# A new order for the first five units, and sums and a norm that leave GpSimd

## The chip, the cores and the metric

The kernel runs on one core of a Trainium2 chip. The metric is the device time of one execution in microseconds (us). Engines are called by their names in the profile: PE (TensorE matmul), PEld (its weight loads), DVE (VectorE), ACT (ScalarE), POOL (GpSimd) and SP (the queue that issues all DMAs of this kernel).

## The reference, cut to what matters

A transformer block on 16 sequences of 256 tokens with 256 features: an attention with 16 heads of 128, and a gated feed-forward layer of width 2048 whose weights come as packed 4-bit codes with scales. Each half is normalised at both ends.

```python
def _layernorm(x):                       # eps 1e-5
    return (x - mean(x)) / sqrt(var(x) + eps)

def attn(x):                             # x: 16 x 256 x 256
    q, k, v = (einsum('bpd,hde->bphe', x, W) + b for W, b in ...)
    s = einsum('bqhe,bkhe->bhqk', q, k) / sqrt(128)
    a = softmax(where(causal, s, -1e5))
    z = einsum('bkhe,bhqk->bqhe', v, a)
    return einsum('bqhe,hed->bqd', z, W_O) + b_O

def ffn(x):                              # Wg, Wu, Wd: 4-bit codes times scales
    gate, up = x @ Wg.T, x @ Wu.T
    return (gelu_tanh(gate) * up) @ Wd.T

x = x + _layernorm(attn(_layernorm(x)))
x = x + _layernorm(ffn(_layernorm(x)))
```

## The kernel before, in words

**Precision.** TensorE multiplies in fp32r. To keep fp32 accuracy, operands are split into a high part (a copy to fp32r) and a low part (value minus high part). A product takes three matmuls (`mm3`): high by high, low by high and high by low. So nearly every operand costs a copy on ScalarE (the high part) and a subtraction on VectorE or GpSimd (the low part): `kh`/`kl`, `qh`/`ql`, `vh`/`vl`, `ph`/`pl`, `zh`/`zl`, `inter`, and the weights.

**Attention.** The 4096 tokens are cut into `NBLK` = 8 blocks of 512 (two sequences). For each block there are 8 pairs of heads, and a *unit* is one head of one block: 128 units. The loop `for i in range(-5, N + 2)` is a software pipeline over units; step `i` runs, in this order, stages of different units:

- `st_s(i+4)`: scores of both sequences into the two `sc` banks; four masked minima on VectorE in place; the waiting `vl` (kept in the list `after`); four exponentials on ScalarE, which read the `sc` banks; reciprocals `rc`; four scalings `pr` on GpSimd.
- `st_qk(i+5)`: the products `pk` and `pq` (six matmuls each, one PSUM bank each), then `kh`, `kr`, `qh`, `qr` on ScalarE and `kl`, `ql` on VectorE.
- `st_t(i+4)`: the block transpose `tr` of `pr` on VectorE.
- `st_o`, `st_z(i)`, `st_p(i+1)`: the output product `po`, the product `pz` with the values, and the split of the transposed probabilities `ph`, `pl`.
- `st_v(i+4)`: the value product `pv` of four heads for one quarter of the tokens. There is one `pv` bank; ScalarE copies it to `vh` (or `vr`), and for the first two of four quarters VectorE forms `vl`, which is put on the list `after` and issued by the next `st_s`, behind its masks.
- `st_b`, `st_w`: the DMA hop through HBM that completes the transpose (`hop`, `pt`).

In the first five steps (`i` = -5 to -1) there is no `pz` and no `po`, so TensorE has only `sc`, `pk`, `pq` and `pv`.

**Order on each engine.** The helper `run` (line 99) records each instruction behind the last one of every engine, so on each engine the program's order is the order in which it runs; all instructions have line 99 in the profile, and groups are told apart by tile names. The DMAs are recorded in order as well (line 91).

**Side work.** Jobs that are not part of the pipeline (weight splits, norms, weight decoding, operand sums) are generators in lanes: `splits`, `urgent`, `behind`, `made`, `spare`, `idle`. A job says with `yield V_`, `A_`, `G_` or `N_` on which engine its next piece runs. A `slot(kinds)` takes one piece of the first lane whose next piece is of that kind and due. `add` puts a job into a lane, `await_` and `finish` drain one.

- `mid(b, oT)`: the end of attention for a block. It turns the output, loads it (`o`), measures it (`ln_stats`: VectorE, with one power on GpSimd), normalises it (`att`, four pieces), adds the input (`xs`, two sums), stores it to `x1d`, measures again, normalises again (`xn`, four pieces) and hands the turned tokens on for the feed-forward stage.
- `x_ops(sb)`: for each pair of blocks (`NSB` = 4 pairs), the operands of the feed-forward products. The stage uses Winograd's form of Strassen's method: seven block products (`m1` to `m7`) instead of eight, with sums of the four input blocks. `less` makes a sum, `put` splits one (a copy on ScalarE and a subtraction).
- `end(b, tr)`: the end of the feed-forward half for a block: norm on ScalarE in place in `o`, and the residual sum into `X1`, four sums of 256 columns.

**Feed-forward stage.** From about 1035 us on a loop runs over 32 groups `k` (4 pairs of blocks by 8 slices of the width). A group takes 15 us, with the products `pa`, `pf`, `pd`, `pe` for gate and up (`g`, `u`), the sums and the gelu that turn them into `inter`, and four down products `st_d` of the group before. It has five places with `slot(V_)` followed by `slot(A_ + G_)`.

At the start 30 transposes (`keep_warm(30)`) into a scratch bank keep TensorE busy before the first tokens have come, with 3 and 6 more among the first real ones.

Of the kernel before, what the change touches and what calls it, by code (L numbers as in the profile page):

```python
# [28 lines left out]
def kernel(  # L29
# [30 lines left out]
    def f(ap):  # L60
        return ap.bitcast(F32)
# [24 lines left out]
    def dma(dst, src):  # L86
        if queue[0] is None:
            queue[0] = nc.sync.dma_start(dst, src).ins
            return
        with tc.issue_after(queue[0]):  # L90
            queue[0] = nc.sync.dma_start(dst, src).ins
# [3 lines left out]
    def run(op, dst, *args, **kw):  # L95
        with ExitStack() as behind:
            for m in last.values():
                behind.enter_context(tc.issue_after(m))
            ins = op(dst, *args, **kw)  # L99
        last[ins.ins.engine] = ins.ins  # L100
        return ins
# [49 lines left out]
    def half(t, b, hf):  # L151
        r = b * TB + hf * S
        return t[r : r + S, :].rearrange("(t p) d -> p t d", p=P)
# [18 lines left out]
    def pairs_of_h(ap, out):  # L172
        return ap.rearrange("p (two h) -> p two h" if out else "p (h two) -> p two h", two=2)

    def ln_apply(dst, src, mv, rs, t):
        run(nc.gpsimd.tensor_scalar, dst, src, mv[:, t, 0:1], rs[:, t : t + 1], ALU.subtract, ALU.mult)
# [17 lines left out]
    def wide(name):  # L194
        return work.tile([P, 4, D], F32, tag="wide", name=name, bufs=4)
# [135 lines left out]
    def w_get(p, n):  # L331

        if p < NG:
            add(splits, split(p, n), A_ if n in "vo" else V_)
        elif p < len(pairs):
            overdue(now[0] + 4)
            if n == "v":
                key, part = p // 2, p % 2
                w = HALF.pop(key) if part else w_tile(n)
                HALF[key] = w  # L340
                dma(f(w[:, part]), WD[key % (NG // 2), n][:, part])
                if part:
                    W[key, n] = w_view(HALF.pop(key))
            else:
                w = w_tile(n)
                dma(f(w), WD[p % NG, n])
                W[p, n] = w_view(w)
# [200 lines left out]
    def cols4(ap):  # L548
        return ap.rearrange("p (h k j) -> p h k j", h=2, k=4)
# [3 lines left out]
    def mid(b, oT):  # L553

        tr = back_tile()
        back(tr, 0, oT[:, 0])
        yield V_
        back(tr, 1, oT[:, 1])
        yield N_, 2
        o = yield from back_load(tr)  # L560
        xs = [x_load(x, b, hf) for hf in range(2)]
        yield V_, 8
        xt = [xs[t // 2][:, t % 2, :] for t in range(4)]
        mv, rs = yield from ln_stats(o)
        att = wide("att")
        for t in range(4):
            yield G_
            ln_apply(cols4(att[:, t, :]), o[t], mv, rs, t)
        for hf in range(2):
            yield G_  # L570
            run(nc.gpsimd.tensor_tensor, xs[hf], xs[hf], att[:, 2 * hf : 2 * hf + 2, :], ALU.add)
        yield V_
        mv, rs = yield from ln_stats(xt)
        for hf in range(2):
            dma(half(x1d, b, hf), xs[hf])
        xn = wide("xn")
        for t in range(4):
            yield G_
            ln_apply(pairs_of_h(xn[:, t, :], True), pairs_of_h(xt[t], False), mv, rs, t)
        yield V_  # L580
        HOP2[b] = dram.tile([P, 4, 2 * P], F32, name=f"xhop{b}")
        yield from turn_tokens(HOP2[b], xn)
        ready.add((0, b))
# [108 lines left out]
    def x_ops(sb):  # L692

        xr = []
        for b in (2 * sb, 2 * sb + 1):
            xr.append(wide("xr"))
            dma(xr[-1], HOP2[b])
        yield A_, 8

        def block(kt, bb):  # L700
            return xr[bb].rearrange("p a (m i) -> p m a i", m=8)[:, 4 * kt : 4 * kt + 4]

        def four(ap):
            return ap.rearrange("p (t a i) -> p t a i", t=4, a=4)

        ops = X[sb] = {}

        def put(name, hi, lo, src):
            run(nc.scalar.copy, four(hi), src)
            run(nc.gpsimd.tensor_tensor, four(lo), src, f(four(hi)), ALU.subtract)  # L710
            ops[name] = hi, lo

        def pair():
            t = work.tile([P, 2, 2, TB], F32R, tag="xT", name="xT", bufs=4)
            return [(t[:, 0, k], t[:, 1, k]) for k in range(2)]

        def less(o, a, b):
            run(nc.gpsimd.tensor_tensor, o, a, b, ALU.subtract)

        x11, x12, x21, x22 = block(0, 0), block(0, 1), block(1, 0), block(1, 1)  # L720
        p1, p2 = pair()
        put("11", *p1, x11)
        yield A_
        put("21", *p2, x21)
        yield G_
        t1, t3, t4 = x11, x12, x21
        less(t1, x12, x11)
        yield G_
        less(t3, x22, x12)
        yield G_  # L730
        t2 = four(sb_tile("raw", "xsum", 6))
        less(t2, x22, t1)
        yield A_
        p1, p2 = pair()
        put("t2", *p1, t2)
        yield G_
        less(t4, t2, x21)
        yield A_
        put("t1", *p2, t1)
        yield A_  # L740
        w = w_tile("k")
        put("t3", w[:, 0], w[:, 1], t3)
        yield A_
        w = w_tile("q")
        put("22", w[:, 0], w[:, 1], x22)

        def last_one():
            hi = work.tile([P, TB], F32R, tag="ph", name="xh")
            lo = work.tile([P, TB], F32R, tag="pl", name="xl")
            put("t4", hi, lo, t4)  # L750

        if sb == 0:

            ops["last"] = last_one
        else:
            yield A_
            last_one()

    def sb_tile(tag, name, bufs):
        return work.tile([P, TB], F32, tag=tag, name=name, bufs=bufs)  # L760
# [127 lines left out]
    def end(b, tr):  # L888
        o = yield from back_load(tr)
        yield V_, 8  # L890
        mv, rs = yield from ln_stats(o)
        yield V_
        nb = ln_shift(mv, rs, 4)
        for t in range(4):
            yield A_
            run(nc.scalar.activation, o[t], o[t], AF.Identity, bias=nb[:, t : t + 1], scale=rs[:, t : t + 1])
            to = cols4(X1[b][t // 2][:, t % 2, :])
            run(nc.gpsimd.tensor_tensor, to, to, o[t], ALU.add)
        yield N_, 2
        for hf in range(2):  # L900
            dma(half(out, b, hf), X1[b][hf])
# [86 lines left out]
    def keep_warm(count):  # L988
        for n in range(count):
            run(nc.tensor.transpose, warm[:, n % 4, :], ident, ident)  # L990

    keep_warm(30)
    add(urgent, first, V_)
    finish(urgent)
    run(nc.gpsimd.tensor_scalar, bqs, bqk[:, 0, :], qscale, 1.0, ALU.mult, ALU.mult)
    for p in range(2):
        w_split(p, "v")
    for p, n in (2, "v"), (1, "k"), (1, "q"):
        w_get(p, n)

    def weights(*of):
        for pn, n in of:
# [3 lines left out]
    for i in range(-5, N + 2):  # L1006
        p = i // 2
        odd = i % 2 == 1
        if p >= 0 and not odd and p < len(pairs):
            b, g = pairs[p]  # L1010
            if g == 0 and b + 1 < NBLK:
                add(urgent, ln1(b + 1), N_)
            if b == 0 and g == 6:
                pieces = [(fg, n) for fg in range(NG) for n in "gud"]
                f_load(*pieces[0])
            if b == 0 and g == 7:
                for m, piece in enumerate(pieces):
                    add(idle, f_make(*piece, pieces[m + 1] if m + 1 < len(pieces) else None), V_)
            if b == NBLK - 1 and g == 0:
                add(spare, x_ops(0), N_)  # L1020
        if 0 <= i + 4 < N:
            st_s(i + 4)
        slot(V_)
        if i + 5 < N:
            st_qk(i + 5)
        slot(V_, urgent, behind)
        slot(G_)
        slot(G_)
        if 0 <= i + 4 < N:
            st_t(i + 4)  # L1030
        if i == N:
            X[0].pop("last")()
        if i >= N - 4:
            part(0, ("m1", "m2", "m6", "m5", "m7", "m3")[i - (N - 4)])
        if 0 <= p - 1 < len(pairs):
            st_o(p - 1, i % 2)
        if 0 <= i < N:
            st_z(i)
        if 0 <= i + 1 < N:
            st_p(i + 1)  # L1040
        if 0 <= i + 4 < N:
            st_v(i + 4)
        elif after:
            run(*after.popleft())
        if 0 <= i + 3 < N:
            st_b(i + 3)
        if 0 <= i + 4 < N:
            st_w(i + 4)
        if odd:
            weights((p + 1, "o"), (p + 5, "v"))  # L1050
        else:
            weights((p + 4, "k"), (p + 4, "q"))
        slot(A_ + G_)
        if N - 9 <= i < N - 7:
            f_get(0, "ug"[i - (N - 9)])
# [97 lines left out]
```

## Time and profile before

| | before |
|---|---|
| time, median of 3 runs | 1522.82 us (1521.78 to 1523.2) |
| profiled execution | 1522.04 us |
| its span in the profile | 1520.3 us |
| PE busy | 1501.7 us (99%) |
| PEld / DVE / ACT / POOL busy | 1278.5 / 1175.9 / 1033.9 / 810.3 us |
| DMA | 407.55 MB, mean 268 GB/s |
| granted PE clock, mean | 0.999 |

The profile shows one execution. Times in it are counted from the start of the span. "Idle before" is the idle time of an engine just before an instruction, with the instruction that ended it behind an arrow. A row of the timeline gives start, duration, engine, line, operation, output and inputs, shapes and count; rows of a group by shape give count, busy time, mean of one in ns, and idle time before. A table by stretch gives each engine's busy time in it with the number of instructions, then the granted clock of TensorE, the share of DMA time and the GB/s.

### The profile page before, as it was taken

The numbers are of one execution on the slowest core, as the hardware profiler recorded it, in microseconds if no ns is written. First come the engines' busy times: TensorE is split into PE (matmuls) and PEld (weight loads), VectorE is DVE, ScalarE is ACT, GpSimd is POOL, SyncE is SP. The second block draws the span as 40 slices with busy tenths as digits, with TensorE's granted clock in tenths as the row PEclk, the third lists the DMA queues.
The fourth block names the chain that finished last, engine by engine and source line by source line (L and its number), as shares of the span: only waits on it lengthen the run. The fifth ranks groups of instructions, "written<-read, shape, count | busy, mean of one in ns | idle before, by whom it ended". The sixth has DMA issues, their size and how long they took to land.

```text
span 1520.3 us, 25782 instructions
## 1 busy us (share of the span) xinstructions
PE 1501.7 (99%) x7831; PEld 1278.5 (84%) x7831; DVE 1175.9 (77%) x2950; ACT 1033.9 (68%) x2606; POOL 810.3 (53%) x1018
## 2 busy tenths in 40 slices
PE   8999999999999999999999999999999999999997
PEld 7888888888888888888888888887788878878886
DVE  6876787787787888788778777777877777787766
ACT  6886776777676677676776767675666665666565
POOL 3754578677667776866876876882320230140100
PEclk9999999999999999999999999999999999999999
DMA  8998899999889899899899999976547465645551
GB/s 287 336 317 266 263 310 298 294 299 317 281 291 329 280 322 311 265 322 299 280 287 304 312 304 316 310 247 254 219 180 276 185 232 195 254 174 201 216 232 57
DMA packets 200427, 407.55 MB, mean 268 GB/s; under 512 B 21472, under 2 KB 128480, under 8 KB 189536
## 3 DMA queue, kind: packets, MB, share of 16 engines
q1 hardware_dynamic: 200288, 405.91, 79.6%
q8 instruction: 62, 1.02, 0.3%
q14 instruction: 77, 0.63, 0.1%
HBM read 294.15 MB, written 111.67 MB: 267 GB/s over the span
## 4 chain that ended last, share of the span: by engine, by line
PE 89%; DVE 5%; ACT 4%; DMA 1%; issue 1%; POOL 1%; POOLq 0%; ACTq 0%; SPq 0%; DVEq 0%
PE pd L99 11%; PE pk L99 11%; PE po L99 11%; PE pv L99 11%; PE pq L99 11%; PE pz L99 10%; PE sc L99 9%; PE pa L99 7%; PE pf L99 5%; DVE sum L99 3%; PE pe L99 2%; DVE inter L99 1%; ACT inter L99 1%; ACT part L99 1%; ACT o L99 1%
## 5 line engine op out<-in xcount | busy, mean ns | idle before, releaser
L99 POOL TENSOR_SCALAR pr<-pr,rc 128x128 f32<-128x128 f32 (+1 forms) x512 | 250.2, 504 | 89.9 <-DVE rc L99 89.9
L99 ACT ACTIVATE pr<-sc,mn 128x128 f32<-128x128 f32 (+1 forms) x512 | 208.2, 419 | 87.2 <-DVE mn L99 87.0
L99 POOL TENSOR_TENSOR pl<-pt,ph 128x512 fp32r<-128x512 f32 x128 | 165.0, 1289 | 190.1 <-ACT ph L99 181.8
L99 DVE CUSTOM_DVE_ANT_0 sc<-sc,mask 128x128 f32<-128x128 f32 (+1 forms) x512 | 180.6, 373 | 67.8 <-PE sc L99 59.1
L99 PE MATMUL pv<-wv,xT 128*128 128x512 f32 x768 | 208.9, 407 | 0.0
L99 PE MATMUL pd<-inter,wd 128*128 128x512 f32 (+1 forms) x792 | 199.7, 386 | 2.7 <-DVE inter L99 1.4
L99 ACT ACTIVATE zh<-pz,bqk 128x512 fp32r<-128x512 f32 x128 | 88.3, 690 | 167.3 <-PE pz L99 167.2
L99 PE MATMUL pk<-xT,wk 128*128 128x512 f32 x768 | 199.4, 395 | 0.3 <-POOL xT L99 0.2
L99 PE MATMUL pq<-xT,wq 128*128 128x512 f32 x768 | 196.3, 391 | 0.0
L99 POOL TENSOR_TENSOR rs<-rs,mhalf 128x4 f32<-128x4 f32 (+1 forms) x35 | 35.9, 1026 | 283.9 <-DVE rs L99 277.5
L99 PEld LDWEIGHTS pd<-inter,wd 128*128 128x128 f32 x792 | 144.2, 188 | 38.6 <-DVE inter L99 6.5
L99 PEld LDWEIGHTS pq<-xT,wq 128*128 128x128 f32 x768 | 144.2, 188 | 32.8
L99 PE MATMUL po<-zh,wo 128*128 128x512 f32 x512 | 157.7, 389 | 0.0
L99 PEld LDWEIGHTS pk<-xT,wk 128*128 128x128 f32 x768 | 134.9, 188 | 23.8 <-POOL xT L99 0.7
L99 PEld LDWEIGHTS pv<-wv,xT 128*128 128x128 f32 x768 | 135.0, 189 | 23.6
L99 ACT COPY part<-pa 128x512 f32<-128x512 f32 x192 | 111.5, 584 | 62.7 <-PE pa L99 60.3
L99 DVE SCALAR_TENSOR_TENSOR zl<-pz,bqk,zh 128x512 fp32r<-128x512 f32 x128 | 95.8, 749 | 73.7 <-ACT zh L99 73.6
L99 ACT CAST inter<-sum 128x512 fp32r<-128x512 f32 x128 | 80.1, 626 | 100.0 <-DVE sum L99 99.9
L99 DVE TENSOR_TENSOR inter<-sum,inter 128x512 fp32r<-128x512 f32 x128 | 93.2, 728 | 58.9 <-ACT inter L99 56.0
L99 DVE STREAM_TRANSPOSE tr<-pr 128x768 f32<-128x768 f32 x128 | 123.3, 963 | 1.7 <-POOL pr L99 1.2
L99 DVE SCALAR_TENSOR_TENSOR kl<-pk,bqk,kh 128x512 fp32r<-128x512 f32 x128 | 96.1, 751 | 30.7 <-ACT kr L99 26.7
L99 PEld LDWEIGHTS po<-zh,wo 128*128 128x128 f32 x512 | 96.0, 188 | 19.9
(138 smaller groups left out, 3779.6 us busy)
## 6 DMA issues: line engine op xcount, KB each, us to landing
hop<-tr SPq DMA_DIRECT2D x512, 96.0 KB
pt<-hop SPq DMA_DIRECT2D x128, 384.0 KB
wk<-wk SPq DMA_DIRECT2D x64, 512.0 KB
wq<-wq SPq DMA_DIRECT2D x64, 512.0 KB
wo<-wo SPq DMA_DIRECT2D x64, 512.0 KB
wu<-fu SPq DMA_DIRECT2D x32, 1024.0 KB
wg<-fg SPq DMA_DIRECT2D x32, 1024.0 KB
wv<-wv SPq DMA_DIRECT2D x56, 512.0 KB
```

What stands on the lines that cost most here:

```text
L99: ins = op(dst, *args, **kw)
```

## The change

It has two parts. In the first five steps, `st_qk(i+5)` and two slots for weight splits now come ahead of `st_s(i+4)`; the first pieces of weights are asked for in another order (`w_get(2, "v")` moves to the end of step -4), and 27 transposes stand where 30 stood. In the second part, work moves off GpSimd: `mid` of the last block runs its two norms on ScalarE and its sums on VectorE (`beside`); `x_ops(1)` to `x_ops(3)` run their sums and subtractions on VectorE, each piece in a slot of its own; and `end` adds the residual on VectorE, in slots of its own. `x_ops(0)` keeps GpSimd.

```diff
 def mid(b, oT):
...
+        beside = b == NBLK - 1
+        if beside:
+            yield V_
+            nb = ln_shift(mv, rs, 4)
         for t in range(4):
-            yield G_
-            ln_apply(cols4(att[:, t, :]), o[t], mv, rs, t)
+            yield A_ if beside else G_
+            if beside:
+                ln_apply_act(cols4(att[:, t, :]), o[t], nb, rs, t)
+            else:
+                ln_apply(cols4(att[:, t, :]), o[t], mv, rs, t)
         for hf in range(2):
-            yield G_
-            run(nc.gpsimd.tensor_tensor, xs[hf], xs[hf], att[:, 2 * hf : 2 * hf + 2, :], ALU.add)
+            yield V_ if beside else G_
+            engine = nc.vector if beside else nc.gpsimd
+            run(engine.tensor_tensor, xs[hf], xs[hf], att[:, 2 * hf : 2 * hf + 2, :], ALU.add)
...
         for t in range(4):
-            yield G_
-            ln_apply(pairs_of_h(xn[:, t, :], True), pairs_of_h(xt[t], False), mv, rs, t)
+            yield A_ if beside else G_
+            to, src = pairs_of_h(xn[:, t, :], True), pairs_of_h(xt[t], False)
+            if beside:
+                ln_apply_act(to, src, nb, rs, t)
+            else:
+                ln_apply(to, src, mv, rs, t)
 def x_ops(sb):
...
-        yield A_, 8
+        yield N_, 8
...
+        engine = nc.vector if sb else nc.gpsimd
+        D_ = V_ if sb else G_
+
         def put(name, hi, lo, src):
+            yield A_
             run(nc.scalar.copy, four(hi), src)
-            run(nc.gpsimd.tensor_tensor, four(lo), src, f(four(hi)), ALU.subtract)
+            if sb:
+                yield V_
+            run(engine.tensor_tensor, four(lo), src, f(four(hi)), ALU.subtract)
             ops[name] = hi, lo
...
         def less(o, a, b):
-            run(nc.gpsimd.tensor_tensor, o, a, b, ALU.subtract)
+            yield D_
+            run(engine.tensor_tensor, o, a, b, ALU.subtract)
...
 def end(b, tr):
...
             run(nc.scalar.activation, o[t], o[t], AF.Identity, bias=nb[:, t : t + 1], scale=rs[:, t : t + 1])
+            yield V_
             to = cols4(X1[b][t // 2][:, t % 2, :])
-            run(nc.gpsimd.tensor_tensor, to, to, o[t], ALU.add)
+            run(nc.vector.tensor_tensor, to, to, o[t], ALU.add)
...
-    keep_warm(30)
+    keep_warm(27)
...
     for p in range(2):
         w_split(p, "v")
-    for p, n in (2, "v"), (1, "k"), (1, "q"):
-        w_get(p, n)
+    for n in "kq":
+        w_get(1, n)
...
     for i in range(-5, N + 2):
...
+        if i < 0:
+            st_qk(i + 5)
+            for _ in range(2):
+                slot(V_, splits)
         if 0 <= i + 4 < N:
             st_s(i + 4)
         slot(V_)
-        if i + 5 < N:
+        if 5 <= i + 5 < N:
             st_qk(i + 5)
...
         if 0 <= i + 4 < N:
             st_w(i + 4)
+        if i == -4:
+            w_get(2, "v")
```

More of the change, by code (lines that the diff above doesn't have):

```diff
@@ L575, in mid @@
             dma(half(x1d, b, hf), xs[hf])
+        if beside:
+            yield V_
+            nb = ln_shift(mv, rs, 4)
         xn = wide("xn")
         for t in range(4):
-            yield G_
-            ln_apply(pairs_of_h(xn[:, t, :], True), pairs_of_h(xt[t], False), mv, rs, t)
+            yield A_ if beside else G_
+            to, src = pairs_of_h(xn[:, t, :], True), pairs_of_h(xt[t], False)
+            if beside:
+                ln_apply_act(to, src, nb, rs, t)
+            else:
+                ln_apply(to, src, mv, rs, t)
         yield V_
@@ L717, in less @@
         def less(o, a, b):
-            run(nc.gpsimd.tensor_tensor, o, a, b, ALU.subtract)
+            yield D_
+            run(engine.tensor_tensor, o, a, b, ALU.subtract)
         x11, x12, x21, x22 = block(0, 0), block(0, 1), block(1, 0), block(1, 1)
         p1, p2 = pair()
[L722 to L725, printed above, removed]
+        yield from put("11", *p1, x11)
+        yield from put("21", *p2, x21)
         t1, t3, t4 = x11, x12, x21
[L727 to L730, printed above, removed]
+        yield from less(t1, x12, x11)
+        yield from less(t3, x22, x12)
         t2 = four(sb_tile("raw", "xsum", 6))
-        less(t2, x22, t1)
-        yield A_
+        yield from less(t2, x22, t1)
         p1, p2 = pair()
[L735 to L740, printed above, removed]
+        yield from put("t2", *p1, t2)
+        yield from less(t4, t2, x21)
+        yield from put("t1", *p2, t1)
         w = w_tile("k")
-        put("t3", w[:, 0], w[:, 1], t3)
-        yield A_
+        yield from put("t3", w[:, 0], w[:, 1], t3)
         w = w_tile("q")
-        put("22", w[:, 0], w[:, 1], x22)
+        yield from put("22", w[:, 0], w[:, 1], x22)
         def last_one():
@@ L749, in last_one @@
             lo = work.tile([P, TB], F32R, tag="pl", name="xl")
-            put("t4", hi, lo, t4)
+            yield from put("t4", hi, lo, t4)
         if sb == 0:
-            ops["last"] = last_one
+            ops["last"] = lambda: deque(last_one(), maxlen=0)
         else:
-            yield A_
-            last_one()
+            yield from last_one()
     def sb_tile(tag, name, bufs):
@@ L896, in end @@
             run(nc.scalar.activation, o[t], o[t], AF.Identity, bias=nb[:, t : t + 1], scale=rs[:, t : t + 1])
+            yield V_
             to = cols4(X1[b][t // 2][:, t % 2, :])
-            run(nc.gpsimd.tensor_tensor, to, to, o[t], ALU.add)
+            run(nc.vector.tensor_tensor, to, to, o[t], ALU.add)
         yield N_, 2
@@ L1031 @@
         if i == N:
+            await_(X[0], "last", spare)
             X[0].pop("last")()
```

## The prediction

> **What bounds the kernel now.** I read the page's engine shares and chain first.
>
> ```profile
> PE 1501.7 (99%) x7831; PEld 1278.5 (84%) x7831; DVE 1175.9 (77%) x2950; ACT 1033.9 (68%) x2606; POOL 810.3 (53%) x1018
> PE 89%; DVE 5%; ACT 4%; DMA 1%; issue 1%; POOL 1%; POOLq 0%; ACTq 0%; SPq 0%; DVEq 0%
> ```
>
> TensorE is busy for 1501.7 of 1520.3 us, and the diff leaves every real matmul in place. So only its 18.6 idle us can be won, and whatever makes TensorE wait is lost. Next, the busy time by stretch.
>
> ```profile
> core 0: us, PE busy (x) PEld busy (x) DVE busy (x) ACT busy (x) POOL busy (x), PEclk, DMA share, GB/s
> 9.90:42.10 32.20, 26.72 (x135) 21.62 (x136) 23.31 (x66) 24.08 (x69) 12.27 (x20) 1.00 0.91 304
> 42.10:1000.00 957.90, 957.66 (x5378) 833.47 (x5378) 756.93 (x2209) 683.24 (x1932) 679.77 (x889) 1.00 0.92 300
> 1120.00:1210.00 90.00, 90.00 (x395) 73.55 (x394) 67.97 (x120) 56.33 (x105) 10.89 (x12) 1.00 0.59 219
> 1210.00:1225.00 15.00, 14.25 (x62) 11.17 (x61) 12.64 (x16) 8.85 (x17) 7.59 (x5) 1.00 0.51 193
> 1332.00:1347.00 15.00, 14.27 (x62) 11.17 (x61) 12.45 (x16) 9.05 (x17) 7.59 (x5) 1.00 0.50 193
> 1513.50:1516.30 2.80, 0.00 (x0) 0.00 (x0) 2.74 (x12) 1.69 (x4) 0.88 (x2) 1.00 0.48 162
> 1516.40:1520.00 3.60, 0.00 (x0) 0.00 (x0) 0.28 (x1) 0.82 (x2) 0.00 (x0) 0.50 0.45 148
> ```
>
> 5.5 us are idle in the first units, 0.2 in the next 958 us, about 0.75 in each of two 15 us stretches where GpSimd works for 7.6. Who ends the early waits (the waits of TensorE up to 45 us), and how one early unit runs (the timeline, other rows left out):
>
> ```profile
> PE sc L99 <- ACT qr L99: 5.4, 4, 2.2
> ```
>
> ```profile
> 21.73 0.48 DVE L99 SCALAR_TENSOR_TENSOR ql<-pq,bqs,qh 128x256 fp32r<-128x256 f32 x1
> 21.75 0.49 PE L99 MATMUL sc<-kr,qr 128*128 128x128 f32 x2 [2.18 <-ACT qr L99]
> 22.13 0.97 DVE L99 STREAM_TRANSPOSE tr<-pr 128x768 f32<-128x768 f32 x1
> 24.50 0.69 DVE L99 TENSOR_TENSOR vl<-pv,vh 128x512 fp32r<-128x512 f32 x1
> 25.35 0.82 POOL L99 TENSOR_SCALAR pr<-pr,rc 128x128 f32<-128x128 f32 x2 [3.77 <-DVE rc L99]
> 25.79 1.52 PE L99 MATMUL pv<-wv,xT 128*128 128x512 f32 x6
> ```
>
> Scores wait for qr. But see vl: it comes after the masks of the next scores, and pv (one PSUM bank) may be overwritten only then. Today pk and pq lie between sc and pv and hide that. Last, VectorE's sums by shape: 1140 to 1170 us, GpSimd quiet, and then 1211 to 1222, GpSimd busy.
>
> ```profile
> L99 DVE TENSOR_TENSOR sum<-sum 128x512 f32<-128x512 f32 x8 | 5.5, 684 | 1.2 <-ACT sum L99 1.2
> L99 DVE TENSOR_TENSOR inter<-sum,inter 128x512 fp32r<-128x512 f32 x8 | 5.5, 684 | 3.5 <-ACT inter L99 3.4
> ```
>
> ```profile
> L99 DVE TENSOR_TENSOR sum<-sum 128x512 f32<-128x512 f32 x3 | 4.3, 1420 | 0.0
> L99 DVE TENSOR_TENSOR inter<-sum,inter 128x512 fp32r<-128x512 f32 x3 | 2.7, 903 | 0.9 <-ACT inter L99 0.7
> ```
>
> The same instruction takes 684 or 1420 ns. Those reading PSUM (sum<-pd,part) stay at 678.
>
> **Part 1, the first five units.** The new TensorE order is qk0 qk1 sc0 pv0 qk2 sc1 pv1 qk3 sc2 pv2 qk4 sc3 pv3 sc4. VectorE's is, per step, kl ql, two weight remainders (steps -5, -3, -1), masks, vl, rc, tr. I lay it out from intervals of the trace. pk's start to kh 1.66 us; kh to kr 0.58, kr 0.47, then kl 0.72; pq's start to qh 1.63, qr ends 0.86 later, then ql 0.40; a weight remainder 0.61; scores to first mask 1.01, all masks 1.48, vl 0.65; first mask to exponentials 0.88, their end 1.7 later; rc to pr 0.25, four pr 1.65; tr 0.89; groups on TensorE: qk 2.73, sc 1.15, pv 1.38.
>
> - keep_warm 27 for 30: 3 x 0.21 us (30 take 6.44): pk0 starts at 9.3 instead of 9.94.
> - pk1 waits for kl0 (12.8), sc0 starts at 15.6, masks 17.2 (after ql1), exponentials 18.1, rc 19.05 and 19.8, pr until 20.95, tr0 21.0 to 21.9.
> - tr0 now stands ahead of kl2 on VectorE. So kl2 21.9, ql2 22.6, two remainders until 24.3, masks of sc1 until 25.75, vl0 until 26.4. TensorE has finished sc1 at 22.0 and waits 4.4 us for pv1.
> - pk3 27.8, pq3 29.2, ql3 31.75, masks of sc2 32.15 to 33.65, vl1, pv2 at 34.4: idle 2.7.
> - pk4 35.8, ql4 39.65, remainders, masks of sc3 41.3. pv3 waits for ScalarE's vr alone (36.6), but sc4 needs sc3's banks, read by the exponentials at 43.0: sc4 starts at 43.0, against 40.72 (idle 2.0).
> - Then tr3 (45.0) delays masks 4 to 45.9, qr5 ends at 50.2 and sc5 starts there (before 47.48); tr4 and zl0 delay masks 5, sc6 at 57.8 (before 53.96). From there po lengthens a unit and covers the rest: sc7 65.7 (before 61.85).
>
> Loss: **3.8 us**, the 0.6 from keep_warm already in it. Bounds: 2.3 (sc4 alone) to 5. The moved split of wv 2 takes away ScalarE's 2.88 us wait for its raw load at 16.75; the layout holds that already. Its load, the raw wk and wq of pair 2 and 3 and their stores go to SP some us earlier or later; in front of them wait the hop writes for tr. I cost this at nothing, because no DMA ends a wait of TensorE up to 45 us, and the first pt, issued at 27.87, is read by ph only at 40.52; without that cover its 384 KB would cost 1.3 us at the 304 GB/s of this stretch.
>
> A row speaks on the clock too: it stays 1.00 through the 2.18 us gap at 21.75 and falls to 0.50 at 1516.3, 2.8 us after the last matmul. A gap of 4.4 lies beyond both. The cold start shows the price: transposes 0.21 apart until 7.6 us, half that later. Some 3 to 6 us at half rate would cost 1.5 to 3; the moment looks bound to more than the gap's length, so from 0 to 3 I take 0.8, nearer to the long quiet early row. The Trainium skill (TensorE: Matmul & The Clock Gate, Part 1) speaks against this change: an idle window of about 3.4 us halves the clock, in windows that run freely. By it alone the sum would take 0 or about 1.7; the trace's 2.8 us is shorter than its window.
>
> **Part 2, work off GpSimd.** From 1040 us on GpSimd loses 33 operand sums (1.29 to 1.75 us each), 24 residual sums (0.78), 4 att, 4 xn (1.25 to 1.39) and 2 xs sums (1.29). VectorE gains 35 of 0.69 (0.61 back to back) and 24 of about 0.41: 31 us. ScalarE gains 8 of 0.61 (row o<-o).
>
> What goes: GpSimd's interference. A late inter shows it: at 1217 six pd matmuls that would have ended at 1218.5 let the next group start at 1219.8, 1.3 us late, and the same at 1340. Around 1066, 1081 and 1097 such groups are 0.6, 0.5 and 0.5 late. Together 4.2 us.
>
> What comes: in a group of 15 us VectorE has gaps. The critical chain is part copy, cast (ScalarE 1155.36), inter (VectorE 1156.02 to 1156.71), pd at 1156.72: no slack. The cast waits for a sum that ends 0.7 us earlier where nothing is added. Of five VectorE slots per group three fall into gaps of 0.8 to 1.4 us, one behind that sum, and one, between u's product and the pe sums, delays it by 0.6 of the 0.7. Four oback transposes of 0.71 in the group at 1140 did so at no TensorE idle. Head of line: a moved put waits for its ScalarE copy, issued a slot earlier; sums queue behind it. I charge 0.5 us in all (bounds 0 and 7). The block's ScalarE norms fall into its 0.9 us gaps: nothing. Sum: **-3.7 us** (-4.5 to +3). SP carries the same DMAs.
>
> x_ops(0) keeps GpSimd; its first steps shift by a slot: nothing, as part forces them.
>
> **Sum.** The profiled execution took 1522.04 us, span 1520.3 and 1.7 around it. +3.8 +0.8 -3.7 = +0.9. The median is 0.8 above that execution: 1522.8 + 0.9 = 1523.7.
>
> **Rivals.**
> - Slower (0.15): VectorE becomes the bound in the feed-forward stage. For it: 67.97 of 90 us busy, and 6 us back to back before each cast. It decides once the moved work delays that sum by over 0.7 us: a put whose copy is late takes 0.61 + 0.6 of waiting, 0.5 too much, in two slots of some 7 groups 7 us. With the 4.2 won, part 2 is +2.8: 1522.8 + 4.6 + 2.8 = 1530. Against: the oback group.
> - Faster (0.18): the order does what it is for, the 5.4 us wait for qr goes and pv waits for nothing: 1522.8 - 5.4 - 0.6 - 3.7 = 1513. For it: the waits name qr alone. Against: vl behind the masks.
> - The clock falls at pv1 (0.25): 3.0 in place of 0.8: 1522.8 + 3.8 + 3.0 - 3.7 = 1526.
> - Likeliest (0.42): both parts as sized, 1521 to 1525.5.
>
> **Numbers.** A measurement of this kernel tells about 0.2% (3 us) from no change: faster is under 1519.8, slower over 1525.9. Likeliest all within, the clock case half over, the VectorE case over, the remainder faster; of the likeliest's edges a little goes over: faster 0.18, same 0.47, slower 0.35. The range 1517.5 to 1528 leaves out most of the faster rival and the worst VectorE case.
>
> **What would show it.** Right: the first units' waits name sc<-qr hardly, but pv<-DVE vl, 4 and 2.7 us; pk5 2.4 us later; sum<-sum near 690 ns at 1210 to 1225 and no idle there; residual sums on DVE at 0.4. Wrong: sc4 before 40 us, or pd<-inter waits in the groups of operand sums.

## The result, and the profile after

| kernel | median (lowest to highest), us | ratio to the kernel before, 95% interval |
|---|---|---|
| before, timed beside it | 1521.96 (1521.37 to 1523.2) | |
| after | 1527.93 (1526.78 to 1528.34) | 1.0037 (1.0026 to 1.0047) |

The change costs 6.0 us, where the prediction had 0.9. The profiled execution took 1528.24 us, with a span of 1526.4. Its engine shares and the first line of its chain:

```profile
PE 1503.2 (98%) x7828; PEld 1281.7 (84%) x7828; DVE 1186.8 (78%) x3011; ACT 1038.0 (68%) x2614; POOL 728.0 (48%) x951
PE 94%; DVE 3%; ACT 1%; DMA 1%; POOL 1%; issue 1%; POOLq 0%; DVEq 0%; ACTq 0%; SPq 0%
```

GpSimd is 82 us less busy, VectorE 11 more. VectorE took over work that the prediction put at 31 us; the rest of the difference is that its own sums got shorter (from 1040 us on sum<-sum takes 685 ns on average, 765 before). The span grew by 6.1 us: TensorE is busy for 1.5 us more, with the same products to do, and idle for 4.6 us more. The busy time by stretch, with three short stretches of the first units added:

```profile
core 0: us, PE busy (x) PEld busy (x) DVE busy (x) ACT busy (x) POOL busy (x), PEclk, DMA share, GB/s
9.90:42.10 32.20, 24.95 (x111) 20.19 (x110) 18.02 (x50) 19.06 (x53) 8.85 (x15) 0.89 0.88 300
42.10:1000.00 957.90, 955.55 (x5363) 831.55 (x5362) 756.36 (x2203) 682.10 (x1930) 675.62 (x885) 1.00 0.92 299
22.91:26.32 3.41, 0.26 (x1) 0.26 (x2) 3.10 (x12) 1.78 (x9) 0.15 (x1) 1.00 0.76 161
26.32:29.73 3.41, 3.41 (x9) 2.64 (x9) 1.15 (x2) 1.03 (x4) 1.48 (x4) 0.50 0.96 341
1120.00:1210.00 90.00, 90.00 (x398) 74.22 (x397) 72.08 (x131) 56.78 (x106) 1.98 (x2) 1.00 0.61 227
1210.00:1225.00 15.00, 15.00 (x68) 12.43 (x67) 11.65 (x22) 11.20 (x22) 0.03 (x1) 1.00 0.46 179
1332.00:1347.00 15.00, 15.00 (x68) 12.43 (x67) 11.65 (x22) 11.16 (x21) 0.00 (x0) 1.00 0.47 176
```

Two things are to be seen. In the two stretches of 15 us where GpSimd worked before, it is now empty and TensorE has no idle time: part 2 does what it says. And in the first units TensorE is not only idle for 7.3 of 32.2 us (5.5 before): its granted clock, 1.00 before, is 0.89. The row 26.32:29.73 shows where: TensorE is busy throughout, at half clock.

The waits of TensorE, and the three early ones in its timeline:

```profile
PE pv L99 <- DVE vl L99: 6.7, 2, 4.2
PE sc L99 <- ACT pr L99: 2.1, 1, 2.1
PE pa L99 <- DMA wu<-fu: 1.5, 1, 1.5
```

```profile
26.06 2.72 PE L99 MATMUL pv<-wv,xT 128*128 128x512 f32 x6 [4.21 <-DVE vl L99]
35.66 2.19 PE L99 MATMUL pv<-wv,xT 128*128 128x512 f32 x6 [2.47 <-DVE vl L99]
46.29 0.49 PE L99 MATMUL sc<-kr,qr 128*128 128x128 f32 x2 [2.11 <-ACT pr L99]
```

The wait for qr (5.4 us before) is gone and the waits for vl and for the exponentials stand in its place: 4.21, 2.47 and 2.11 us, where the layout by hand had 4.4, 2.7 and 2.0. The six matmuls of pv1 take 2.72 us, where six took 1.52 in the kernel before. New and not predicted is a wait of 1.5 us at 1057, for a weight load.

VectorE's sums at 1211 to 1222 us, by shape:

```profile
L99 DVE TENSOR_TENSOR sum<-sum 128x512 f32<-128x512 f32 x3 | 2.1, 686 | 1.0 <-ACT sum L99 1.0
L99 DVE TENSOR_TENSOR inter<-sum,inter 128x512 fp32r<-128x512 f32 x3 | 2.1, 689 | 0.8 <-ACT inter L99 0.8
```

1420 ns became 686, and 903 became 689.

### The profile page after: what moved, and what is told of

Same layout as the page of the kernel before. It is cut to its first block, busy times and chain, and to the rows that moved or that the text cites. A ratio compares the mean times of both kernels' runs of the same rounds, so it can differ in the third digit from the quotient of the medians.

```text
span 1526.4 us, 25748 instructions
## 1 busy us (share of the span) xinstructions
PE 1503.2 (98%) x7828; PEld 1281.7 (84%) x7828; DVE 1186.8 (78%) x3011; ACT 1038.0 (68%) x2614; POOL 728.0 (48%) x951
## 4 chain that ended last, share of the span: by engine, by line
PE 94%; DVE 3%; ACT 1%; DMA 1%; POOL 1%; issue 1%; POOLq 0%; DVEq 0%; ACTq 0%; SPq 0%
PE pd L99 13%; PE pk L99 12%; PE pv L99 11%; PE pq L99 11%; PE po L99 11%; PE pz L99 10%; PE sc L99 9%; PE pa L99 8%; PE pf L99 5%; PE pe L99 2%; DVE sum L99 1%; DMA wu<-fu 1%; PE warm L99 0%; DVE sc L99 0%; DVE inter L99 0%
## 5 line engine op out<-in xcount | busy, mean ns | idle before, releaser
L99 DVE TENSOR_TENSOR inter<-sum,inter 128x512 fp32r<-128x512 f32 x128 | 89.0, 696 | 57.4 <-ACT inter L99 56.4
```

## The experiments

All times are medians, each beside the kernel before on the same chip (1522.2, 1522.4, 1522.5, 1522.4 and 1522.9 us in five groups of runs; after stands beside 1521.96). A difference between runs of two groups carries this spread.

| run | what it is | us | ratio, 95% interval |
|---|---|---|---|
| e1 | part 1 alone | 1531.45 | 1.0060 (1.0047 to 1.0073) |
| e2 | part 2 alone | 1518.55 | 0.9976 (0.9966 to 0.9985) |
| e3 | after, the three early waits filled | 1523.21 | 1.0007 (0.9998 to 1.0016) |
| e4 | after, vl ahead of the next products | 1521.21 | 0.9993 (0.9984 to 1.0001) |
| e5 | after, the first wait filled | 1524.87 | 1.0016 (1.0007 to 1.0025) |
| e6 | e4, its last early wait filled | 1520.97 | 0.9991 (0.9982 to 0.9999) |
| e7 | after, one load later on SP | 1525.92 | 1.0021 (1.0011 to 1.0030) |
| e8 | operand sums alone | 1518.85 | 0.9972 (0.9960 to 0.9983) |
| e9 | after, VectorE's early order mended | 1523.49 | 1.0004 (0.9995 to 1.0013) |
| e10 | e9, one step further | 1523.54 | 1.0005 (0.9996 to 1.0014) |
| e11 | e9, loads of pt later | 1520.09 | 0.9984 (0.9975 to 0.9993) |
| e12 | e10, e11 and e7 together | 1518.88 | 0.9975 (0.9964 to 0.9985) |

**e1 and e2: each part alone.** e1 is the kernel before with part 1 of the diff, e2 with part 2.

> Part 1 alone: the new order of the first five units on the kernel before; GpSimd keeps its work. My theory (the loss sits in pv waiting for vl, in sc waiting for the exponentials, and in a clock halved three times after these waits): TensorE waits of about 4.2, 2.5 and 2.1 us for pv, pv and sc, three clock drops, the steady state entered 7 us later, 1522 + 7 = 1529 us. Rival (the two parts spoil each other, the order alone is what its name says): the wait of 5.4 us for qr goes and the time falls to about 1516. Rival (the loss comes from the feed-forward stage): no change, 1522.

> Part 2 alone: the sums and the norm off GpSimd, the old order of the first units. If the part is worth what the prediction said: 1522 - 3.7 = 1518. If what it showed in the changed kernel belongs to it (0.8 us won, with a wait of 1.5 us for the DMA wu that is new): 1521, with that wait in the trace near 1050. If the DMA wait belongs to where in the program an instruction fetch falls, and not to the moves: no such wait, 1518 to 1519. Rival (VectorE becomes the bound): over 1525.

Measured: +9.2 and -3.7 us against the runs beside them. e1's trace has after's three early waits and three falls of the clock, and a wait of 1.6 us for wu, which the expected 1529 did not hold. Their sum, +5.5, is close to the +6.0 of both, so the parts hardly touch each other. Part 2 is worth what the prediction gave it. Part 1 costs 4.6 us more than the 4.6 it was given.

**e3: the same order, no empty TensorE.** Dummy transposes into the scratch bank fill the three waits.

```diff
+        if i == 0:
+            keep_warm(16)
         if 0 <= i + 4 < N:
             st_s(i + 4)
+        if i in (-3, -2):
+            keep_warm(36 if i == -3 else 20)
```

> The changed kernel with dummy transposes in the three waits of TensorE (36 behind the second scores, 20 behind the third, 16 ahead of the fifth), so that it waits as before but works meanwhile. If the halved clock is what made 3.8 us into 7: no drop of the clock in the first 60 us, the wait for vl replaced by transposes, 3 us less than the changed kernel, about 1525. If slow matmuls only fill time that would be waited anyway: the clock stays up and the time is that of the changed kernel, 1528.

The timeline of TensorE in e3 shows the filler, and what is left of each wait:

```profile
22.36 4.09 PE L99 MATMUL warm<-ident 128*128 128x128 f32 x36
26.74 1.65 PE L99 MATMUL pv<-wv,xT 128*128 128x512 f32 x6 [0.28 <-DVE vl L99]
32.10 2.35 PE L99 MATMUL warm<-ident 128*128 128x128 f32 x20
34.73 1.66 PE L99 MATMUL pv<-wv,xT 128*128 128x512 f32 x6 [0.28 <-DVE vl L99]
41.50 1.91 PE L99 MATMUL warm<-ident 128*128 128x128 f32 x16
43.75 0.49 PE L99 MATMUL sc<-kr,qr 128*128 128x128 f32 x2 [0.34 <-ACT pr L99]
```

The filler ends 0.3 us ahead of what it waits for, so it delays nothing: vl and the exponentials come when they came before. But pv1 takes 1.65 us and not 2.72, the clock stays at 1.00, and the time falls by 4.7 us. The wait for wu is not there either, so this run alone does not price the clock; e7 takes the two apart. Against e2 of the same group, which has the old order, e3 costs 4.7 us: that is the layout's loss without the clock.

**e5: only the first wait filled.** Of e3's filler the 36 transposes at step -3 stay.

> The kernel after, with 36 dummy transposes on TensorE in the first of its new waits only (the 4.2 us one ahead of pv1); the waits of 2.5 us (pv2) and 2.1 us (sc4) keep TensorE empty. In the kernel after the granted clock fell three times, at 26.3, 36.6 and 46.8 us, 3.41 us each. Theory 'each quiet stretch costs its own drop': the first drop goes, the two behind the 2.5 and 2.1 us waits stay, a third of the about 3 us is won back: 1526.8. Rival 'the long wait starts it' (a wait of over 4 us is needed, the later two drops only follow it): no drop is left at all, unit 4's scores start near 44 us in place of 46.3, and the time is 1523 to 1525.4, by whether the later wait for a weight load (2.1 us) stays.

Two stretches of its table, each followed by the next:

```profile
31.65:35.06 3.41, 0.99 (x4) 0.85 (x5) 2.53 (x12) 1.72 (x8) 0.88 (x3) 1.00 0.93 312
35.06:38.47 3.41, 3.41 (x9) 2.65 (x9) 0.98 (x1) 0.59 (x1) 0.76 (x2) 0.50 0.92 367
41.89:45.30 3.41, 1.31 (x9) 0.84 (x7) 2.63 (x11) 1.72 (x9) 0.35 (x1) 1.00 0.60 166
45.30:48.71 3.41, 3.41 (x13) 2.86 (x12) 2.19 (x9) 1.94 (x6) 3.41 (x6) 0.50 0.92 344
```

The first fall is gone, the other two are there, behind waits of 2.47 and 2.10 us. So each fall has its own cause and needs no wait of 4 us. The first feed-forward product starts at 1012.84 us instead of 1014.42, which prices that fall at 1.6 us (pk0 starts at 8.8 us in both). The time alone would fit the rival; the falls in the trace speak against it. The time is 1.9 us below the expectation, and the wait for wu, which e5 lacks too, is worth that (e7).

**e4 and e6: the same wait, with and without a fall.** In e4 the first five steps issue the waiting vl ahead of the next products; e6 adds 20 transposes ahead of unit 4's scores.

```diff
         if i < 0:
+            while after:
+                run(*after.popleft())
             st_qk(i + 5)
...
+        if i == 0:               # e6 alone
+            keep_warm(20)
```

> The changed kernel, but in the first five steps the waiting vl is issued at the start of the next step, ahead of kl, ql, the weight remainders and the masks. If vl behind the masks is the cause: the first wait of pv falls from 4.2 to under 1 us, the second stays at 2 to 3 (vl then waits for vh behind the exponentials), one clock drop at most is left, and the time is 5 to 6 us below the changed kernel, about 1522. If the cause is elsewhere (weights, SP): the waits move on to another stage and the time stays at 1527 to 1528.

> The kernel after with vl ahead of the next products in the first five steps (as in the run that took 1521.2) and 20 dummy transposes in its last early wait, the 2.87 us ahead of unit 4's scores. Theory 'clock': that wait brings the one drop of 6.83 us at 39.2, worth about 3.3; filled, there is no drop, unit 5's scores start near 46 in place of 49.2, and the time is 1518. Rival 'order': unit 5's scores are late because VectorE and ScalarE are behind, whatever the clock: they start at 48 or later and the time stays at 1520.5 to 1521.5.

e4 is 6.7 us faster than after. Some 2 of these are the wait for wu, of which e4 has 0.2 us left; the rest is in the first units, where vl behind the masks was the greater part of the loss, as the prediction's reading of the timeline had it: the first feed-forward product starts at 1009.11 us instead of 1014.42. e4's clock falls once, behind the wait of 2.87 us for the exponentials. e6 fills that wait, and there the clock holds, but it falls in another place. Both kernels wait 1.9 us ahead of pv2, from 28.1 to 30.0, with the same instructions up to there. First e4, then e6:

```profile
28.93:32.34 3.41, 2.33 (x10) 1.94 (x11) 3.34 (x11) 1.45 (x6) 0.68 (x1) 1.00 1.02 391
35.76:39.17 3.41, 1.18 (x6) 0.62 (x4) 3.34 (x11) 1.36 (x5) 0.00 (x0) 1.00 0.97 338
39.17:45.99 6.82, 6.17 (x20) 5.31 (x21) 3.47 (x15) 5.36 (x21) 5.34 (x10) 0.50 0.98 350
```

```profile
27.32:30.73 3.41, 1.53 (x10) 1.24 (x9) 2.45 (x5) 2.61 (x6) 2.29 (x4) 1.00 1.00 348
30.73:34.14 3.41, 3.41 (x10) 2.66 (x9) 2.11 (x11) 2.19 (x9) 1.04 (x3) 0.50 1.02 338
```

In e6 the wait lies in one stretch of 3.41 us and leaves TensorE 1.53 us of work in it, 45%: the clock falls. In e4 it is cut by a boundary at 28.93, and the stretch behind holds 2.33 us, 68%: the clock stays. It is the share of a fixed stretch that decides, not the wait's length. The expectation of 1518 for e6 failed in part by that fall (1.6 us by e5's price) and by a wait of 0.5 us for wu; the last 0.9 us is open. Its unit 5 starts at 47.82, between the two theories' 46 and 48, which settles nothing about the order.

**e7: one load behind three others.** The output of the last attention block (`o` from `ohop`, and `xs`) is loaded four slots later, which puts the loads of wd, wg and wu ahead of it on SP and moves no other transfer past another.

```diff
-        yield N_, 5
+        yield N_, due            # 9 for the last block, 5 otherwise
         o = wide("o")
         dma(o, hop)
```

> The kernel after, with the last attention block's output loaded (o from ohop, and xs) four slots later, so that on SP the three weight loads of the next feed-forward group stand ahead of it; nothing else moves. Theory 'SP queue': in the kernel after this load waited on SP for its hop's writes until 1044.6 and held the three weight loads, and pa waited for wu twice, 2.1 us in all: those waits go, 1525.8. Rival 'the DMA engines': the loads are late because the transfers themselves are slow there, whatever stands ahead: pa still waits for wu, 1527.9.

SP's timeline, after and then e7:

```profile
1038.85 1.77 SPq L91 DMA_DIRECT2D ohop<-oback  x4
1044.56 0.34 SPq L91 DMA_DIRECT2D o<-ohop  x1
1044.95 0.94 SPq L91 DMA_DIRECT2D xs<-in_x  x2
1046.91 0.45 SPq L91 DMA_DIRECT2D wu<-fu  x1
```

```profile
1040.11 1.77 SPq L91 DMA_DIRECT2D ohop<-oback  x4
1042.96 0.39 SPq L91 DMA_DIRECT2D wu<-fu  x1
1044.35 0.32 SPq L91 DMA_DIRECT2D o<-ohop  x1
```

wu is issued 2.85 us after the hop instead of 8.06, pa waits for no load, and the time is 1525.92 where 1525.8 was expected. So SP's order is what held wu. It cost 2.0 us by these times, and 2.4 by the traces, in which the time from the first feed-forward product to the end of the span falls from 511.98 to 509.54 us. (The expectation's 2.1 us of waiting is more than the trace of after names: 1.5 for wu and 0.2 for wg.) Why the hop took 5.7 us until the load behind it could go (3.9 in the kernel before) is open: an instruction fetch of 16 KB lies among its packets, but one lies near the hop in the kernel before too, and e3 and e5 have the same stage without the wait. That was not tried.

**e8: the operand sums alone.** The kernel before with the `x_ops` part of the diff; the last block's norm and the residual sums stay on GpSimd.

> The kernel before with the move of the operand sums (x_ops 1 to 3) to VectorE alone; the last block's norm and the residual sums stay on GpSimd, the first five units keep their order. Theory of the prediction: the gain is the interference of the operand sums with VectorE's own, 4.2 less 0.5; all of part 2's 3.7 us is here: 1518.5. Rival: it is spread over the three moves by their GpSimd time (33 operand sums of about 1.4 us are 46 us, residual sums 19, last norm and its sums 13): some 59% here, 1520.0.

-3.6 us, against -3.7 for all of part 2. The sums at 1211 to 1222 us, by shape:

```profile
L99 DVE TENSOR_TENSOR inter<-sum,inter 128x512 fp32r<-128x512 f32 x4 | 2.8, 690 | 1.4 <-ACT inter L99 1.3
L99 DVE TENSOR_TENSOR sum<-sum 128x512 f32<-128x512 f32 x4 | 2.7, 683 | 0.4 <-ACT sum L99 0.4
```

The gain sits where GpSimd's work collided with VectorE's, not where GpSimd saved time: the other two moves are worth nothing that can be told. Two things go with that. A residual sum collides too: beside one, at 1193.68 us in e8, sum<-part takes 1.07 us instead of 0.68, and still its move won no time. And e8's trace has a wait that e2's has not:

```profile
PE pa L99 <- DMA wu<-fu: 1.3, 2, 1.1
```

So the operand sums alone may be worth up to a microsecond more than -3.6, and the other two moves may cost as much.

**e9 to e12: can the order be made to pay?** e9 repairs VectorE's order in the first five steps: vl behind its own copy, tr and its hop behind the next masks. e10 also puts unit 5's products ahead of unit 4's scores.

```diff
+        early = i < 0            # e10: i < 1
+        if early:
             st_qk(i + 5)
...
             st_s(i + 4)
+        if early and i < 0 <= i + 4:
+            st_v(i + 4)
+            while after:
+                run(*after.popleft())
...
+        if 0 <= i + 3 < 4:       # one step later than before
+            st_t(i + 3)
+            st_w(i + 3)
...
```

> The kernel after with VectorE's and ScalarE's order mended in the first five steps: the value product comes right behind the scores, vl is issued behind its own copy and not behind the next masks, and the transpose tr with its hop goes one step later, behind the next masks. Theory 'vl and tr make the loss': pv waits for vl under 1 us in all, units follow at about 5.7 us, unit 4's scores start near 38 (before 40.7, after 46.3), the first feed-forward product comes some 2 us earlier than before, and with the 3.7 us of the moves the time is 1516 to 1518. Rival 'the first units are bound by work or weights': whatever the order, ScalarE, VectorE and the loads of the first weights hold them at 6.5 us a unit; unit 4's scores start at 41 or later and the time is 1518.5 to 1521.

> As the run before this one, with the sixth step in the new order too: the products of unit 5 come ahead of the scores of unit 4 and fill the wait for unit 3's exponentials (2.1 us in the kernel after). Theory 'vl and tr make the loss': as before this, and the wait ahead of unit 4's scores goes; unit 4's scores near 38 and unit 5's under 45, 1515 to 1517. Rival 'bound by work or weights': 1518.5 to 1521, and the wait only moves to unit 5's scores.

Neither theory held. The lead was there and was lost again. Unit 4's scores start at 38.10, 2.6 us earlier than in the kernel before; unit 6's start at 55.96, 2.2 us later than there (53.80). TensorE's timeline and VectorE's waits from 38 to 66 us in e9:

```profile
38.10 0.49 PE L99 MATMUL sc<-kr,qr 128*128 128x128 f32 x2 [3.27 <-ACT pr L99]
55.96 0.49 PE L99 MATMUL sc<-kr,qr 128*128 128x128 f32 x2 [1.55 <-ACT qr L99]
```

```profile
DVE tr L99 <- DMA hop<-tr: 4.6, 2, 2.5
```

VectorE stands 4.6 us in front of tr, 2.5 of them ahead of unit 6's scores, until an earlier hop has been written and its buffer is free; kl, masks and vl queue behind it. In e10 tr waits 3.8 us at once, TensorE then waits 3.1 us for zl ahead of 52.33, and the clock falls behind that. On SP each pt load stood right behind its own hop. e11 issues the pt loads of units 0 to 2 one step later, and e12 joins e10, e11 and e7.

```diff
-        if 0 <= i + 3 < N:
+        if -2 <= i <= 0:
+            st_b(i + 2)
+        if 3 <= i + 3 < N:
             st_b(i + 3)
```

> The run with tr and vl mended in the first five steps (1523.5) had unit 4's scores at 38.1 and lost its lead by unit 6: tr waited 2.5 and 2.1 us for the writes of an earlier hop, and on SP each pt load stood right behind its own hop. Here the pt loads of units 0 to 2 go one step later, behind the next hop. Theory 'SP queue': tr no longer waits for hop, unit 6's scores start near 51.5 in place of 56.0 and the time falls to 1517 to 1519. Rival 'transfers': the hops are late because the DMA engines are full of weights in this stretch; tr waits as before and the time stays near 1523.

> What the runs point to, together: the run with the later pt loads (1520.1), with unit 5's products ahead of unit 4's scores as well (they fill the 3.3 us wait behind which its clock fell), and with the last output's load four slots later (its pa waited 1.0 us for wu). Theory 'waits and clock': no fall of the clock, unit 5's scores at 45 and unit 6's at 51.5, no pa wait: 1516.5 to 1518, level with or under the moves alone (1518.5). Rival 'the lead is given back': with the leading order kept one unit longer, VectorE, ScalarE or the hops hold units 5 to 7; the first feed-forward product comes no earlier than in the kernel before, and the time is 1519 to 1521.

In e11 the wait for hop is gone and the time falls by 3.4 us, so the queue was the cause of that wait. The time is still above the expected 1517 to 1519, and unit 6's scores start at 53.25 us, not near 51.5: one fall of the clock (behind the 3.3 us ahead of unit 4's scores) and 1.0 us of waiting for wu are left. e12 has neither, and takes 1518.88. But its first feed-forward product starts at 1007.42, no earlier than in the kernel before (1007.29): unit 6's scores wait 1.5 us for qr again.

```profile
53.84 0.49 PE L99 MATMUL sc<-kr,qr 128*128 128x128 f32 x2 [1.54 <-ACT qr L99]
```

e12 is level with e2 and e8, which keep the old order: there the new order is worth nothing, and the gain is part 2's. Not run was e11 with its one fall filled and its wait for wu gone. By e5's 1.6 us and its own 1.0 us that would take about 1517.5 (an estimate), so a gain of a microsecond is not ruled out.

## Why the prediction was right or wrong

The time lies in the range, 0.07 us under its upper end, and on the side that had 0.35. The predicted 1523.7 was 4.2 us too low. That the time is inside is luck: 2.0 us of it come from a wait that no bound of the range had counted.

**The layout: right.** The waits came where and as long as laid out. Its loss, 3.8 us predicted, is 4.7 by times (e3 against e2). In the traces e3's first feed-forward product is 4.6 us later than before's, and 0.7 of that is a later start (its first scores come at 15.95, after's at 15.27): 3.9. Unit 4's scores start at 43.75 us in e3, 43.1 with that start taken off, where the layout had 43.0. The 0.6 us that 27 transposes for 30 were to win, a part of the 3.8, does not show: pk0 starts at 8.8 to 9.5 us in the traces with 27, and at 9.1 to 9.9 in the three with 30.

**The clock: the step that failed.** The sum took 0.8 us, "nearer to the long quiet early row", because the clock had held through the 2.18 us gap at 21.75. That row was read by the gap's length. Here are the two stretches of 3.41 us that the gap falls into, in the kernel before:

```profile
17.89:21.30 3.41, 1.67 (x8) 1.05 (x6) 1.82 (x5) 3.41 (x12) 2.49 (x5) 1.00 0.59 175
21.30:24.72 3.42, 2.97 (x18) 2.69 (x19) 3.35 (x12) 1.69 (x8) 0.28 (x1) 1.00 0.84 268
```

49% and 87%: a boundary cut the gap, and neither part was thin enough. The row proved less than it was taken to prove. In the kernel after three stretches were filled to 8% (the row 22.91:26.32 above), 28 and 38%:

```profile
33.15:36.56 3.41, 0.94 (x5) 0.77 (x5) 2.63 (x12) 1.72 (x8) 0.78 (x2) 1.00 0.99 379
43.39:46.80 3.41, 1.30 (x8) 0.84 (x7) 2.71 (x11) 1.71 (x8) 0.27 (x1) 1.00 0.56 151
```

The clock fell three times, 3.41 us each, behind waits of 4.21, 2.47 and 2.11 us. By the times it cost 4.7 (after against e3) less 2.0 (e7) = 2.7 us, or 2.5 with each run taken against the kernel before beside it. The rival "the clock falls at pv1", with 0.25 and 1526 us, was the right case; it had one place of three, and its price of 3.0 was near.

The Trainium skill (TensorE: Matmul & The Clock Gate, Part 1) speaks of free-running windows of 3413 ns, and the falls here keep to such a grid. Its rule there, no idle gap of over about 3.4 us, is not enough by these runs: a wait of 1.88 us made the clock fall in e6. The measurement decides.

**SP and the DMAs: the second step that failed.** They were costed at nothing "because no DMA ends a wait of TensorE up to 45 us". That looked only at the first units, and the wait came at 1057, in a queue where three loads stood behind one that waits for a hop. It cost 2.0 us (e7). The diff moves none of these transfers past another. after, e1 (1.6 us), e8 (1.1) and e11 (1.0) have the wait, e4 and e6 have 0.2 and 0.5 of it; e2, e3 and e5 have none, and e3 and e5 differ from after in dummy transposes alone. The stage's place in time does not decide alone: the first feed-forward product starts at 1006.81 us in e2 and at 1006.78 in e8, and only e8 waits. Where its code lies, or what else runs in the stage, may; that is open. There was little room in the kernel before too: it used wu 9.9 us after its issue, while in after and e8 wu came 10.5 us after.

**Part 2: right**, in size (-3.7, measured -3.7) and in cause (e8). In the traces the time from the first feed-forward product to the end of the span is 513.0 us before and 509.9 in e2, so 3.1 us of it lie there. The VectorE rival did not come: the slots of the moved sums stayed in the gaps, and TensorE's waits for VectorE in this stage fell: those of pd for inter from 1.4 us to 0.2, while those of pe for a sum rose from 0.2 to 0.6. The row behind the reading was two states of one instruction. The Trainium skill (SBUF — State Buffer, SBUF: two separate sides) says that a VectorE operation with two SBUF inputs and a GpSimd operation reading SBUF exclude each other for a whole instruction. The rows fit that: 1420 ns with GpSimd at work, 683 to 686 without, and 670 to 689 at all times for sums that read PSUM. How long the one holds the other off was not tried by itself.

**The marks.** sum<-sum came as named. Unit 5's pk was to be 2.4 us later and is 6.3 later (48.33 against 42.05), unit 4's scores were to start at 43.0 and start at 46.29: the excess of 3.3 us is two falls at about 1.6.

**The new sum.** Layout 4.7, clock 2.7, SP 2.0, part 2 -3.7: 1522.0 + 5.7 = 1527.7, measured 1527.9. This is no test, since the four terms are differences of the same runs. e1 is one: the first three terms alone should give 1522.2 + 9.4 = 1531.6, measured 1531.45.

## What to carry to other kernels

Before an order is changed on one engine, lay out what stands behind each of its instructions on the others: here VectorE's queue and SP's queue took back what TensorE's order gave. Price a new wait of TensorE of about 2 us and more at its own length and at what a fall of the clock would cost; a few dummy matmuls in the wait tell the two apart. Look for the same instruction with two durations before moving work off an engine: the gain was in the 33 operand sums, some of which collided with VectorE's, and none that can be told in the other moves, though one of those collided as well.

## What the runs showed of the hardware

- The falls lie on a grid. In each trace the time from the first moment at full clock to a fall is a whole number of 3.413 us (after: 5.84 to 26.32 us is six), and a fall lasts 3.41 or 6.83 us. In all traces of this case, up to 55 us, the 16 stretches at full clock in which TensorE was busy for 8 to 45% were each followed by half clock, and the ones of 49% and more by none. Of the stretches already at half clock, those busy for 33% (e7) and 81% (e4) were followed by another at half clock, those of 85% (e10) and more by full clock.
- Where the grid lies against the program differs from one execution to the next, so by their mean clocks the executions of one kernel differ in the number of falls: of ten executions of e7 the four with a mean clock of 0.995 took 1526.7 us on average, the two with 0.998 took 1524.9. The six of after do not show it as clearly: 1528.0 for three with 0.995, 1527.6 for two with 0.998.
- A load on SP that waits for a hop through HBM held the three loads behind it for 5.7 us after the hop's issue in one kernel and 3.9 in another, with the same transfers.
